# Four layers on one core: the first layer prepared two chunks ahead, norm weights folded, and the feed-forward taps split

## The chip, the cores and the metric

The kernel runs on one core of a Trainium2 chip. A core has five engines that run side by side, each with its own queue: TensorE (PE in the profile, its weight loads PEld), VectorE (DVE), ScalarE (ACT), GpSimd (POOL) and SyncE (SP), which here only starts DMAs. The metric is device time in microseconds, the median of several runs.

## The reference

The input x has shape (4, 64, 128, 128): 4 images, 64 channels, 16,384 pixels. It goes through four layers; the change touches the first and the last.

- Layer 0 is a Mamba block over all 65,536 pixels as one sequence, with 128 inner channels and 16 states, then a linear layer, a norm over the channels, SiLU, and x added.
- Layer 1 is a windowed transform with a small two-layer product in it; layer 2 is two convolutions with a gate.
- Layer 3 is two convolutions, a Mamba block for each image with 64 states between two norms, and a feed-forward part (FFN): 64 to 256 channels, a 3x3 convolution on each channel, GELU, and back to 64.

The Mamba step, cut from the reference:

```python
dA = jnp.exp(d_t[..., None] * A)
h = h * dA + (d_t * u_t)[..., None] * b_t[:, None, :]
y = jnp.einsum('bdn,bn->bd', h, c_t)
```

Around it: xz = norm(t) W; a causal convolution of four taps over the sequence and SiLU give u (the kernel's `xc`); z goes through SiLU and gates y (`sz`); delta, B and C are linear in u, delta with a softplus. In layer 3 the norms have weights and biases: norm(t) = (t - mean) * rstd * ln_w + ln_b. In the last step of layer 3, t + FFN(norm(t)) is formed.

## The kernel before

All in float32. The class `_Mamba` (L144) does the scans of layers 0 and 3.

**Tiling of a scan.** The sequence is cut into chunks of 1,024 tokens (`TC`), 64 chunks in either layer. Channels and states are split: 4 states times 32 channels fill the 128 partitions, so a chunk takes 4 channel quarters (`ND`) times 4 groups of states in layer 0, or times 16 in layer 3. Each (group, quarter) is one iteration: 16 or 64 a chunk. `run` (L412) walks over them in order, and `pin` (L269) ties every engine to that order, so within the two Mamba parts each engine's queue is the order of the program text.

**One iteration.** ACT makes `da` = exp(A * `dl`) (L545), three iterations ahead. The input `bx` lies in PSUM, in two buffers. A group of kind "A" gets it from PE, as eight transposes (L485) of `bxT`, which ACT builds in 28 small multiplications a group (L378) and POOL in one block (L382). A group of kind "D" gets it from DVE (L576), as `du` times B, which PE has spread over the partitions (L491). DVE scans (L582), POOL multiplies by C (L585, `cb`), and PE sums over the states into `y` (L404), two iterations after the group's last scan. Layer 0 has the kinds "DADA", layer 3 "DADAADAADADAADAA".

**Feeds.** What a chunk needs besides is written as generators that `beside` (L465) moves on between iterations. A feed yields "piece" where it has work for PE, of which every iteration's budget allows so many; "wait" k to start k iterations later; or "at" an iteration of its own, which layer 0 gives for each step in the table `slots` (L637), counted from the chunk's first iteration. All pieces of feeds go through one PSUM tile, `pm` (one buffer, L241).

- `ahead`, then `inputs` (L293): in layer 3 first the norm (L1299 to L1320); then z into `sz`, and the convolution and SiLU into `xc`.
- `prepare` (L309): v (delta before softplus, four ACT operations), C (to memory, from which `_C` loads `cb`), B, u, step (three products each half that add up delta, which goes to memory `d2` with delta times u, `dus`), duT (its transposes).
- `replicated` (L493): loads `dl` (five buffers) and `du` (one for each quarter) from `d2`, each spread over the partitions by four DMAs, as soon as their tiles are free. All DMAs stand in SyncE's one queue.
- `behind`: gates y with `sz` into `yg` (L608, on DVE), then the projection, and in layer 3 a norm (L1335 to L1340).

The arguments `leads` of `run` tell how many iterations before its chunk `ahead` and `prepare` start: 28 and 16 in layer 0 (L721), 64 and 36 in layer 3 (L1346). Short-lived tiles share the tag "tmp", six buffers (L290).

**The feed-forward part** (`layer3_ffn`, L1350) goes over 32 strips of 16 rows and is not pinned: the order on each engine is chosen when the program is built, from the program order and dependences. For a strip n, DVE makes nine taps of the 3x3 convolution for channels 128 to 255 (`g1`, L1447 to L1453), GELU follows on ACT (L1454); PE makes the first 128 channels with diagonal weights (`pd`, L1464). Between three taps of PE, `first` (L1390) makes a third of the next strip's hidden channels: PE into `ph` (one buffer, L1417), ACT into `h` (L1422), first t = 0 (PE's channels), then t = 1 (DVE's). Then come the output products (`po`, one buffer, L1483 and L1486) and the sums on DVE (L1490).

## Time and profile before

| what | value |
|---|---|
| median of 3 runs | 19,794.03 us (19,793.55 to 19,795.57) |
| the profiled execution, its time | 19,772.88 us |
| its span in the profile | 19,770.9 us |
| granted TensorE clock | 0.88 |
| busy: PE, DVE, ACT, POOL | 77%, 81%, 75%, 72% of the span |
| layer 0 | 0 to 3,800 us |
| layers 1 and 2, layer 3's convolutions | 3,800 to 6,360 us |
| layer 3's Mamba part | 6,360 to 18,530 us |
| feed-forward part | 18,530 to 19,771 us |
| scans (L582), all | 5,120; 2.34 us each |
| POOL's products (L585), all | 5,120; 2.38 us each |

The profile is of one execution. Its parts are: busy time of each engine; the span in 40 slices; the chain that ended last; groups of equal instructions with their busy time, mean duration, the idle time of their engine ahead of them and who ended it; and DMA issues. An idle engine that is not the bound costs nothing by itself. What follows goes by stage, since each has another limit.

### The profile page before, as it was taken

To read this page: it belongs to the slowest core of one execution; us is meant where nothing else is said; L and a number is where in the kernel's file an instruction comes from. 1 tells how busy PE (TensorE), PEld (TensorE's weight loads), DVE (VectorE), ACT (ScalarE), POOL (GpSimd) and SP (SyncE) were. 2 spreads that over 40 slices of the span, in tenths; PEclk is the share of its full clock that TensorE was granted. 3 is DMA by queue.
4 is the path that set the end of the run, shared out by engine and by line. 5 is a ranking of instruction groups with operands and counts; after the bars stand their busy time and mean duration, and the time that the engine had idled before them with its cause. 6 is when DMAs were issued, how large, how long until landed. Compare 5 with 4: busy or idle time off the path is not lost. (4 is left out here: it accounts for less than half of the span.)

```text
span 19770.9 us, 239165 instructions
## 1 busy us (share of the span) xinstructions
PE 15212.0 (77%) x80176; PEld 7692.9 (39%) x80176; DVE 15957.5 (81%) x8862; ACT 14860.6 (75%) x30365; POOL 14218.6 (72%) x8094
## 2 busy tenths in 40 slices
PE   7787877778897777777777777777777777777777
PEld 3333333367544333333333333333333333333222
DVE  6888888722122999999999999999999999999766
ACT  7888888501223988989889888898988999889522
POOL 6888888600000999999899999999999999889400
PEclk8888888879998888888888888888888888888899
DMA  5555555401122233232332323323233232332211
GB/s 132 146 148 144 149 143 150 129 20 43 32 69 70 75 86 88 75 86 76 86 88 76 86 76 86 88 76 86 76 86 88 76 87 79 83 87 75 58 44 41
DMA packets 669526, 1722.92 MB, mean 87 GB/s; under 512 B 196784, under 2 KB 231936, under 8 KB 660864
## 3 DMA queue, kind: packets, MB, share of 16 engines
q1 hardware_dynamic: 668288, 1707.62, 32.7%
q8 instruction: 629, 10.31, 0.2%
q14 instruction: 609, 4.99, 0.1%
HBM read 1434.27 MB, written 272.63 MB: 86 GB/s over the span
## 5 line engine op out<-in xcount | busy, mean ns | idle before, releaser
L585 POOL TENSOR_TENSOR ring<-ring,cb 128x1024 f32<-128x1024 f32 x5120 | 12094.2, 2382 | 1370.7 <-DVE ring L582 1008.9
L582 DVE TENSOR_TENSOR_SCAN ring<-da,state,bx 128x1024 f32<-128x1024 f32 x4848 | 11133.8, 2334 | 805.6 <-PE bx L485 518.7
L545 ACT ACTIVATE da<-dl,A 128x1024 f32<-128x1024 f32 x5120 | 5858.7, 1144 | 1340.4 <-DVE ring L582 727.7
L378 ACT ACTIVATE bxT<-duT,BT 128x128 f32<-128x128 f32 x21504 | 6758.8, 387 | 0.0
L485 PE MATMUL bx<-cst,bxT 128*128 128x128 f32 x24576 | 4311.6, 329 | 2148.4 <-DVE bx L576 1440.6
L485 PEld LDWEIGHTS bx<-cst,bxT 128*128 128x128 f32 x24576 | 3664.2, 215 | 3975.1 <-DVE ring L582 1603.8
L404 PE MATMUL y<-ring,cst 128*32 128x512 f32 x20480 | 3746.6, 641 | 619.1 <-POOL ring L585 618.0
L576 DVE TENSOR_TENSOR bx<-du,bx 128x1024 f32<-128x1024 f32 x2048 | 2515.1, 1228 | 225.2 <-PE bx L491 89.5
L404 PEld LDWEIGHTS y<-ring,cst 128*32 128x32 f32 x20480 | 572.3, 111 | 2246.1 <-POOL ring L585 1391.1
L1134 PE MATMUL cv<-img,cw 64*64 64x512 f32 x9216 | 1009.5, 595 | 76.7 <-DMA img<-d_x 45.7
L491 PE MATMUL bx<-xc,spread 128*128 128x512 f32 x2048 | 1017.1, 619 | 1.3 <-DVE ring L582 0.7
L1065 POOL TENSOR_TENSOR xs<-xs,cl 128x1024 f32<-128x1024 f32 x32 | 74.9, 2340 | 1078.2 <-DVE cl L1064 1078.2
L1408 POOL MEMSET h<- 128x18 f32 x64 | 8.2, 131 | 1135.3 <-DVE g L1451 795.4
L382 POOL TENSOR_TENSOR bxT<-duT,BT 128x512 f32<-128x512 f32 x768 | 803.5, 1046 | 9.3 <-ACT duT L361 9.3
L1295 POOL MEMSET X<- 64x1 f32 x4 | 0.4, 96 | 1125.9 <-DMA cw<-in_l_conv_wT 1125.9
L1134 PEld LDWEIGHTS cv<-img,cw 64*64 64x64 f32 x9216 | 504.0, 134 | 580.1 <-issue 466.3
L1464 PE MATMUL pd<-h,diag 64*64 64x512 f32 x4608 | 665.4, 624 | 0.7 <-issue 0.7
L582 DVE TENSOR_TENSOR_SCAN ring<-da,bx 128x1024 f32<-128x1024 f32 x272 | 609.6, 2276 | 63.1 <-PE bx L485 46.2
L491 PEld LDWEIGHTS bx<-xc,spread 128*128 128x128 f32 x2048 | 347.9, 189 | 693.8 <-DVE ring L582 385.1
L1451 DVE SCALAR_TENSOR_TENSOR g<-h,dww,g 128x2048 f32<-128x2048 f32 x256 | 601.9, 2351 | 9.2
L1422 ACT ACTIVATE h<-ph,ff_fc_b 128x384 f32<-128x384 f32 (+1 forms) x384 | 199.7, 573 | 541.6 <-PE ph L1417 524.1
L250 PE MATMUL pm<-xc,wC 128*32 128x512 f32 (+1 forms) x512 | 190.2, 832 | 515.7 <-ACT pos L316 513.3
(310 smaller groups left out, 13397.9 us busy)
## 6 DMA issues: line engine op xcount, KB each, us to landing
cb<-c SPq DMA_DIRECT2D x5120, 128.0 KB, 2.8
dl<-d SPq DMA_DIRECT2D x2048, 128.0 KB, 4.4
du<-d SPq DMA_DIRECT2D x2048, 128.0 KB, 4.4
d<-pos SPq DMA_DIRECT2D x128, 512.0 KB, 2.6
d<-dus SPq DMA_DIRECT2D x128, 512.0 KB, 3.0
X<-d_t SPq DMA_DIRECT2D x124, 256.0 KB, 5.3
S<-in_x SPq DMA_DIRECT2D x120, 256.5 KB, 4.9
res<-in_x SPq DMA_DIRECT2D x128, 128.0 KB, 2.9
```

The source lines that it names most:

```text
L378: nc.scalar.activation(t[:, k, q].rearrange("p e j -> p (e j)"), c["duT"][:, k, :], AF.Copy, scale=c["BT"][:, k, n : n + 1])
L382: nc.gpsimd.tensor_mul(t[:, k].rearrange("p q e j -> p q (e j)"), c["duT"][:, k].unsqueeze(1).to_broadcast(shape), c["BT"][:, k, NQ * g : ...
L404: nc.tensor.matmul(c["y"][DD * j : DD * (j + 1), _COLS[h]], K.sel, hc[:, _COLS[h]], start=False, stop=u["g"] == self.ng - 1,)
L485: nc.tensor.transpose(bx[:, P * k : P * (k + 1)], v["bxT"][:, k, :, :, j].rearrange("p q e -> p (q e)"), self.K.eye)
L491: nc.tensor.matmul(bx[:, k], self.spread[v["g"]], v["c"]["xc"][:, k], start=True, stop=True)
L545: nc.scalar.activation(das[nexp], v["c"]["dl"][k], AF.Exp, scale=self.A[:, k, v["g"] : v["g"] + 1])
L576: nc.vector.tensor_mul(bxs[i], u["c"]["du"][j], u["B"])
L582: nc.vector.tensor_tensor_scan(hs, das.pop(i), bxs.pop(i), 0.0 if u["c"].get("reset") else st, ALU.mult, ALU.add)
L585: nc.gpsimd.tensor_mul(hc, hs, u["cb"])
L1134: nc.tensor.matmul(p[i][half[h]], W[half[i], k, :], src[half[i], at : at + 4, dx : dx + WW], start=k == 0, stop=k == 8,)
L1451: nc.vector.scalar_tensor_tensor(g1, tap, wk, g1, ALU.mult, ALU.add)
L1464: nc.tensor.matmul(pd[i][half[h]], diag[half[i], k, :], h0[half[i], r : r + 4, dx : dx + WW], start=k == 0, stop=k == 8,)
```

## The change

**First layer.** `leads` become 45 and 25, and the table of slots is spread anew, so that `prepare` of a chunk runs from 24 to 7 iterations ahead of it, and `inputs` from 43 ahead. Two preparations can now be under way, so `front` becomes a table, and `ahead` of a chunk is ended before that of the next starts. `sz` has four buffers in place of three, "tmp" five in place of six.

**Both Mamba parts.** In `prepare`, B stands after the step instead of before u, and duT follows without a wait of two iterations. `dus` goes into the tile of `u`.

**Norms of layer 3.** The weight of the first norm is applied as scale where ACT copies the centred values, its bias goes through the weights once (`shift`) into the biases of SiLU; where the sequence starts, the two columns of padding hold minus the bias. Weight and bias of the second norm go into the feed-forward part's f1 and b1, once. So L1316 and L1340 go.

**Feed-forward part.** `first` makes t = 1 before t = 0. The taps are a generator: five of the next strip's stand before this strip's outputs, four behind, and the GELU of `g1` stands behind the first half of PE's channels.

```diff
@@ -214,7 +214,7 @@
             nc.sync.dma_start(cols[k], w[k])
-        self.conv_b, self.dt_b = cols["conv_b"], cols["dt_b"]
+        self.conv_b, self.dt_b, self.z_b = cols["conv_b"], cols["dt_b"], 0.0
         self.dD = cp.tile([P, P], F32, name="dD")
@@ -238,6 +238,15 @@
+    def shift(self, b):
+        for k, ws in (("conv_b", self.taps), ("z_b", [self.wz])):
+            pm, col = self.pm(), self.cp.tile([P, 1], F32, name=f"{k}_shift")
+            for i, wt in enumerate(ws):
+                self.nc.tensor.matmul(pm[:, :1], wt, b, start=i == 0, stop=i == len(ws) - 1)
+            self.nc.vector.tensor_scalar(col, pm[:, :1], getattr(self, k), None, ALU.add)
+            setattr(self, k, col)
     def pm(self):
@@ -287,13 +296,13 @@
     def tmp(self, name):
-        return self.wp.tile([P, TC], F32, name=name, tag="tmp", bufs=6)
+        return self.wp.tile([P, TC], F32, name=name, tag="tmp", bufs=self.bufs["tmp"])
...
         nc = self.nc
-        xc, sz = c["xc"], c["sz"] = [self.t(k, self.bufs) for k in ("xc", "sz")]
+        xc, sz = c["xc"], c["sz"] = [self.t(k, self.bufs[k]) for k in ("xc", "sz")]
         yield self.slot(c, "z")
@@ -303,7 +312,7 @@
         nc.scalar.activation(xc, pm, AF.Silu, bias=self.conv_b)
-        nc.scalar.activation(sz, sz, AF.Silu)
+        nc.scalar.activation(sz, sz, AF.Silu, bias=self.z_b)
         nc.scalar.preload_act_table_set(SET6)
@@ -328,16 +337,6 @@
-        yield self.slot(c, "B")
-        BT = c["BT"] = self.wp.tile([P, NB, nst], F32, name="BT", tag="BT")
-        block = [
-            (lambda pm, k=k: pm[:, nst * k : nst * (k + 1)], xc[:, P * k : P * (k + 1)], self.wbc[:, :nst], True, True)
-            for k in range(NB)
-        ]
-        pm = yield from self.piece(block[: NB // 2], block[NB // 2 :])
-        nc.scalar.copy(BT.rearrange("p k n -> p (k n)"), pm[:, : nst * NB])
         yield self.slot(c, "u")
@@ -347,10 +346,20 @@
         nc.sync.dma_start(d2[0], pos)
-        du = self.tmp("dus")
+        du = u
         nc.gpsimd.tensor_mul(du, pos, xc)
         nc.sync.dma_start(d2[1], du)
-        yield self.slot(c, "duT", 2)
+        yield self.slot(c, "B")
+        BT = c["BT"] = self.wp.tile([P, NB, nst], F32, name="BT", tag="BT")
+        block = [
+            (lambda pm, k=k: pm[:, nst * k : nst * (k + 1)], xc[:, P * k : P * (k + 1)], self.wbc[:, :nst], True, True)
+            for k in range(NB)
+        ]
+        pm = yield from self.piece(block[: NB // 2], block[NB // 2 :])
+        nc.scalar.copy(BT.rearrange("p k n -> p (k n)"), pm[:, : nst * NB])
+        yield self.slot(c, "duT")
@@ -514,19 +523,21 @@
         first, second = {}, {}
+        at = -1
         for c in chunks[1:]:
-            at = max(0, per * c["no"] - leads[0])
+            at = max(at + 1, per * c["no"] - leads[0])
             first[at] = c
             second[max(at + 8, per * c["no"] - leads[1])] = c
-        front, early = None, {}
+        front, early = {}, {}
         for i, (u, j) in enumerate(its):
             if i % per == per - 4:
-                finished(front)
+                finished(front.get(u["c"]["no"] + 1))
                 replicated(i - 1)
...
                 finished(early[second[i]["no"]])
-                front = started(self.prepare(second[i]), i)
+                front[second[i]["no"]] = started(self.prepare(second[i]), i)
             if i in first:
+                finished(early.get(first[i]["no"] - 1))
                 early[first[i]["no"]] = started(ahead(first[i]), i)
@@ -634,9 +645,9 @@
     nc = tc.nc
-    slots = {"v": -16, "C": -15, "B": -14, "u": -13, "step": -8, "duT": -6, "z": -23, "conv": -21}
-    slots |= {"project": 21, "rstd": 23, "store": 29}
-    m = _Mamba(ctx, tc, K, 16, w, "DADA", 3, slots)
+    slots = {"z": -43, "conv": -37, "v": -24, "C": -22, "u": -21, "step": -16, "B": -14, "duT": -7}
+    slots |= {"project": 22, "rstd": 23, "store": 29}
+    m = _Mamba(ctx, tc, K, 16, w, "DADA", {"xc": 3, "sz": 4, "tmp": 5}, slots)
     cp, wp = m.cp, m.wp
@@ -718,7 +729,7 @@
     chunks = [{"at": divmod(i * TC, HW), "reset": i == 0} for i in range(B * HW // TC)]
-    m.run(chunks, ahead, behind, (28, 16), [12] * 16)
+    m.run(chunks, ahead, behind, (45, 25), [12] * 16)
@@ -1267,21 +1278,25 @@
     nc = tc.nc
-    m = _Mamba(ctx, tc, K, 64, w, "DADAADAADADAADAA", 2)
+    m = _Mamba(ctx, tc, K, 64, w, "DADAADAADADAADAA", {"xc": 2, "sz": 2, "tmp": 6})
     cp = m.cp
...
     nc.sync.dma_start(woT, w["out_wT"])
-    g1, b1, g2, b2 = (_dup(nc, cp, w[k], f"{k}_") for k in ("ln1_w", "ln1_b", "ln2_w", "ln2_b"))
-    def centred(x, out):
+    g1, b1 = (_dup(nc, cp, w[k], f"{k}_") for k in ("ln1_w", "ln1_b"))
+    m.shift(b1)
+    pad = cp.tile([P, 1], F32, name="pad")
+    nc.vector.tensor_scalar_mul(pad, b1, -1.0)
+    def centred(x, out, scale=1.0):
...
         )
-        nc.scalar.copy(out[0], pm[:, :w])
+        nc.scalar.activation(out[0], pm[:, :w], AF.Copy, scale=scale)
         nc.scalar.activation(out[1], pm[:, :w], AF.Square)
@@ -1304,20 +1319,18 @@
         else:
-            nc.gpsimd.memset(S[:, :2], 0.0)
+            nc.gpsimd.tensor_copy(S[:, :2], pad.to_broadcast([P, 2]))
         xs, sq = m.tmp("nxc"), m.tmp("nsq")
-        yield from centred(c["X"], (xs, sq))
+        yield from centred(c["X"], (xs, sq), g1)
         if c is not chunks[-1]:
...
         yield from m.rstd(sq, eps)
-        nc.gpsimd.tensor_mul(xs, xs, sq)
+        nc.gpsimd.tensor_mul(S[:, 2:], xs, sq)
+        if not t0:
+            nc.gpsimd.tensor_copy(S[:64, 2:3], pad[:64])
+        nc.gpsimd.tensor_copy(tail, S[:, TC:])
         yield "wait", 2
-        nc.vector.tensor_scalar(S[:, 2:], xs, g1, b1, ALU.mult, ALU.add)
-        if not t0:
-            nc.gpsimd.memset(S[:64, 2:3], 0.0)
-        nc.gpsimd.tensor_copy(tail, S[:, TC:])
-        yield "wait", 1
         yield from m.inputs(c, S)
@@ -1336,8 +1349,7 @@
         nc.gpsimd.tensor_mul(o, xs, o)
-        yield "wait", 2
-        nc.vector.tensor_scalar(o, o, g2, b2, ALU.mult, ALU.add)
+        yield "wait", 3
         for h in range(NH):
@@ -1377,6 +1389,13 @@
     nc.sync.dma_start(b1, w["fc1_b"].rearrange("(t q) o -> q (t o)", t=2))
+    g, n = (_dup(nc, cp, w[k], f"ff_{k}") for k in ("ln2_w", "ln2_b"))
+    ph = hp.tile([P, 2, 4, WW], F32, name="ph", tag="ph")
+    for t in range(2):
+        nc.tensor.matmul(ph[:, t, 0, :1], f1[half[0], t, :], n[half[0]], start=True, stop=True)
+    nc.vector.tensor_add(b1, b1, ph[:, :, 0, 0])
+    nc.vector.tensor_scalar(f1, f1, g, None, ALU.mult)
     dwb1 = cp.tile([P, 1], F32, name="dwb1")
@@ -1403,7 +1422,7 @@
         yield
-        for t in range(2):
+        for t in (1, 0):
             himg = H[t] = wp.tile([P, R + 2, RW], F32, name=f"h{t}", tag=f"h{t}")
@@ -1431,17 +1450,8 @@
         pass
-    for n, (b, r0) in enumerate(strips):
-        simg = s3[b].rearrange("c (r w) -> c r w", w=WW)
-        oimg = out[b].rearrange("c (r w) -> c r w", w=WW)
-        h0, h1 = H[0], H[1]
-        H = {}
-        ahead = first(*strips[n + 1], H) if n + 1 < len(strips) else iter(())
-        next(ahead, None)
-        res = wp.tile([P, NK, 4, WW], F32, name="res3", tag="res3")
-        for q in range(R // 4):
-            nc.sync.dma_start(res[half[q % 2], q // 2], simg[:, r0 + 4 * q : r0 + 4 * q + 4, :])
+    def taps(h1):
@@ -1451,7 +1461,22 @@
                 nc.vector.tensor_scalar(g1, tap, wk, None, ALU.mult)
-        nc.scalar.activation(g1, g1, AF.Gelu, bias=dwb1)
+            if k in (4, 8):
+                yield g1
+    for g1 in taps(H[1]):
+        pass
+    for n, (b, r0) in enumerate(strips):
+        simg = s3[b].rearrange("c (r w) -> c r w", w=WW)
+        oimg = out[b].rearrange("c (r w) -> c r w", w=WW)
+        h0 = H[0]
+        H = {}
+        ahead = first(*strips[n + 1], H) if n + 1 < len(strips) else iter(())
+        next(ahead, None)
+        res = wp.tile([P, NK, 4, WW], F32, name="res3", tag="res3")
+        for q in range(R // 4):
+            nc.sync.dma_start(res[half[q % 2], q // 2], simg[:, r0 + 4 * q : r0 + 4 * q + 4, :])
@@ -1472,8 +1497,13 @@
                 nc.scalar.activation(g0[i][:, kk], pd[i], AF.Gelu, bias=dwb[:, i : i + 1])
+            if not kk:
+                nc.scalar.activation(g1, g1, AF.Gelu, bias=dwb1)
         for _ in ahead:
             pass
+        later = taps(H[1]) if H else iter(())
+        g2 = next(later, None)
@@ -1492,6 +1522,8 @@
             nc.sync.dma_start(oimg[:, r0 + 4 * q : r0 + 4 * q + 4, :], o[half[q % 2], q // 2])
+        next(later, None)
+        g1 = g2
```

## The prediction

> **What bounds the kernel now.** I read the stage windows first, because the layers have different limits. An "iteration" below is one scan of 1,024 tokens (L582); layer 0 has 16 per chunk, layer 3 has 64, and there are 64 chunks in each. Columns: window, its length, busy time of PE, PEld, DVE, ACT, POOL.
>
> ```profile
> 0.00:3800.00 3800.00, 2998.06 (x13698) 1399.12 (x13698) 3105.12 (x1679) 3132.67 (x5762) 3031.38 (x1668) 0.87 0.56 143
> ...
> 6360.00:18530.00 12170.00, 9108.58 (x44212) 4598.20 (x44212) 11498.87 (x5884) 10885.08 (x23404) 11023.77 (x6208) 0.88 0.31 82
> 18530.00:19771.00 1241.00, 970.67 (x6164) 289.02 (x6164) 746.66 (x444) 339.37 (x550) 16.71 (x148) 0.90 0.18 43
> ```
>
> Layer 0 is bound by no engine: all four are at about 80%, so hand-offs set it. From 100 to 3560 us a chunk takes 58.0 us. Layer 3's Mamba part takes 190 us a chunk and VectorE is busy 94%. The feed-forward part (FFN) takes 37.57 us a strip (gelu L1454 starts at 18927.12 and again at 18964.68) with PE at 78% and DVE at 60%: a chain sets it. Layers 1 and 2, 3,800 to 6,360 us, are untouched. Idle times "at iteration n" are those of the trace, put to the scan that had started last and averaged over the chunks.
>
> Layer 0, the waits from 100 to 3560 us (us in total, times, longest), then its timeline near 3696 us:
>
> ```profile
> DVE ring L582 <- PE bx L485: 258.0, 141, 18.7
> DVE yg L608 <- remote: 223.4, 58, 4.9
> ...
> ACT da L545 <- DMA dl<-d: 173.7, 102, 3.2
> ```
>
> ```profile
> 3695.40 1.07 PE L250 MATMUL pm<-xc,wC 128*32 128x512 f32 x2 [7.21 <-ACT pos L316]
> ...
> 3696.28 2.74 PE L404 MATMUL y<-ring,cst 128*32 128x512 f32 x6
> ...
> 3699.10 1.23 DVE L608 TENSOR_TENSOR yg<-y,sz 128x1024 f32<-128x1024 f32 x1 [4.11 <-remote]
> ```
>
> At the chunk boundary the C matmul stands in PE's queue until ACT has emptied the single `pm`; the last y sums stand behind it; `yg` waits for them, and the scans stand behind `yg`. The "remote" wait is thus PE's y sums: 223.4 / 58 = 3.85 us a chunk.
>
> Layer 3, groups by line from 7,000 to 18,000 us (58 chunks; after the bar: busy us, mean ns, idle before and who ended it), of DVE and of ACT, then SyncE's queue and ACT at one boundary:
>
> ```profile
> L1316 DVE TENSOR_SCALAR S<-nxc,ln_w__37414,ln_b__37417 128x1024 f32<-128x1024 f32 x58 | 117.1, 2020 | 0.0
> ...
> L1340 DVE TENSOR_SCALAR o<-o,ln_w__37420,ln_b__37423 128x512 f32<-128x512 f32 x58 | 30.3, 522 | 0.0
> ```
>
> ```profile
> L545 ACT ACTIVATE da<-dl,A 128x1024 f32<-128x1024 f32 x3708 | 4243.5, 1144 | 1008.2 <-DVE ring L582 625.7 <-DMA dl<-d 342.2 <-DVE bx L576 33.9
> ```
>
> ```profile
> 12250.58 8.09 SPq L507 DMA_DIRECT2D du<-d  x16
> 12258.80 1.89 SPq L507 DMA_DIRECT2D dl<-d  x4
> ```
>
> ```profile
> 12264.82 1.15 ACT L545 ACTIVATE da<-dl,A 128x1024 f32<-128x1024 f32 x1 [4.08 <-DMA dl<-d]
> ```
>
> `delta` (`pos`) is written out only at iteration 54 (12242.85 us here, L349), so sixteen `du` loads stand ahead of the `dl` loads that the next chunk's first exponentials need. ACT loses 342.2 / 58 = 5.9 us, and then runs without a pause from iteration 2 to 19, where DVE waits.
>
> FFN, one strip:
>
> ```profile
> 18927.12 2.00 ACT L1454 ACTIVATE g<-g,dwb 128x2048 f32<-128x2048 f32 x1 [8.92 <-DVE g L1451]
> ...
> 18930.11 1.65 PE L1417 MATMUL ph<-N,f 64*128 64x384 f32 x4 [6.69 <-ACT h L1422]
> ...
> 18941.14 1.28 DVE L1453 TENSOR_SCALAR g<-h,dww 128x2048 f32<-128x2048 f32 x1 [14.05 <-ACT h L1422]
> ```
>
> The loop is closed: nine taps on DVE, gelu on ACT, the eviction of `h` that stands behind it, PE, the last `h` of t=1, and only then the next taps: 23.5 + 14.05 us.
>
> [...]`e` with a bias column takes 1.09 us from PSUM against 0.99 us for a plain copy. So Copy with scale g1 in place of the copy L1284 costs 0 to 0.1 us. I take 0.
>
> **Layer 0, two chunks ahead.** No instruction is removed from the loop except that `du` reuses `u`. What moves, by iteration of the 16: v 0 to 8, C 1 to 10, u 3 to 11, step 8 to 0, B stays at 2, duT 10 to 9, z 9 to 5, conv stays at 11, project 5 to 6.
> - `yg`: at iteration 0 there is now the step. Its matmuls took 5.4 us (12 of 0.6, overlapping). They fit in iterations 0 to 1 (3.7 us each, D groups, where DVE makes its own input), and the y sums at 1 and 2 stand before B, so they end some 8 us after the boundary; `yg` comes at 9.8. Gain 3.84. This cover is thin, 2 us.
> - Of the 258.0 us that scans wait for transposes, 0.8 us a chunk falls at iteration 4, 1.1 at 5, 2.2 at 13. The first goes with the stall. The second is y's start (L401, 3.3 us of PE) ahead of iteration 5's transposes: stays.
> - At 8 to 11 v, duT, C and conv now take turns in the one `pm`. ACT gets e, pos, exp and ln (4.2 us) there in place of two copies (2.0), C's copy 0.6 and the copy of duT as before. I follow PE and ACT one behind the other: conv ends about 1.2 us later than now, with transposes and scan of iteration 13 behind it. The u op (0.67 us of DVE) moves into that wait: net +0.6.
> - The five `dl` and four `du` tiles are asked for earlier; SyncE issues the same number. 0; it helps ACT by up to 2.9 us (173.7 / 60), which is not on the path.
>
> Sum -3.84 - 0.8 + 0.6 = -4.0 us a chunk, times 62 = -250. The first two chunks now crowd iterations 0 to 12 with two preparations: +15, an estimate from three extra pieces of some 5 us. Layer 0: **-235**. Bounds: +1 us a chunk if the crowding costs all of it, -5.5 if every wait goes: +80 to -350.
>
> **Layer 3, norms in weights.** L1316 and L1340 go: (117.1 + 30.3) / 58 = 2.54 us of DVE a chunk. POOL's multiply writes S directly (2.39 us as before); the pad columns cost 0.2 us at each image's start. These ops lie where ACT is the bound, so alone they would give nearly nothing (ACT waits for DVE only 0.35 us at iterations 8 and 9). But B is now behind the step: in D groups the budget is 2, 2, 2, 1 pieces and 0 in A groups. C is done at 34, so the six pieces of the step fall on 40 to 42 instead of 52 to 54, and B and duT on 43 to 53 (duT was forced at 60). `delta` is out 27 us earlier: each `du` goes when its tile falls free (52 to 55) and the `dl` loads follow the exponentials of 60 to 62 directly, issue 2 + landing 4.4 us, in time. ACT gets its 5.9 us back. DVE's idle time is (437.3 + 119.2 + 30.3) / 58 = 10.1 us; some 3.2 are 0.1 us hand-offs in the 24 D iterations, 2.4 lie at 4 and 5, 2.0 at 13 to 19. I take 3.0 of these last 4.4 as gone. -2.54 - 3.0 = -5.5, times 63 = **-347**. Bounds: -0.5 (ACT still the bound) to -8 (DVE's 177 + 5): -30 to -510.
>
> **FFN.** t=1 first; five of the next strip's taps stand before this strip's outputs, four behind. Then gelu of g1 needs only taps that ended early in the strip, and PE runs on. PE's floor: six blocks of 24 depthwise and 4 `ph` matmuls at 3.58 us (starts 18913.45, 18917.03) and two groups of `po` at some 2.8 (18901.99 to 18904.9): 27.1 us. DVE: 1.29 + 8 x 2.36 + 4 x 0.75 = 23.2 us, below. `po` has one buffer: its second group waits for two outputs (1.5 us) that may stand behind half a tap (1): 29.6 us. -8.0 x 31 = -248, +10 for the first strip's full taps: **-238**. The order here is not pinned but chosen when the program is built; bounds 27.1 to 36.2 a strip: -320 to -40. The scaling of f1 and b1, and `shift`: four small loads, four matmuls of one column and some DVE ops once, +5.
>
> Sum: -235 - 347 - 238 + 5 = -815. From the span of 19,770.9: 18,956. The profiled execution itself took 19,772.88 us, the median of the runs is 21 above that, 23 above the span: **18,980 us**.
>
> **Rivals.**
> 1. All of it comes, at the lower bounds of two layers: -350 - 510 - 300 = 18,635. For it: the idle ACT time. Against: all engines then stand above 90%.
> 2. Layer 3's gain is hidden: `dl` still late, because SyncE's queue waits long for `cb` buffers (POOL state, 14.2 us at the longest) and `dl` stands behind. -30 instead of -347: 19,297.
> 3. FFN's order puts all nine taps ahead of the outputs: 20.2 + 1.5 + 2.8 + three blocks 10.7 + 1.0 = 36.2 us; 19,175.
> 4. Layer 0's crowding at 8 to 13 costs the 4 us again: 19,215.
> 5. Slower: with five `tmp` buffers for six a chunk, the `l` of the chunk after next could take the buffer of `du`, which now lives until duT. ACT's ln then waits for PE's transposes, with all exponentials and bxT behind it, PE waiting for the same `pm`. Before shows no such wait; the code's order says a few us. It decides only from (235 + 580) / 64 = 12.7 us a chunk; at 14 us the result is 19,877.
>
> **How the numbers follow.** Forecast 0.50 (18,830 to 19,130); rival 1 0.13; 2 0.13; 3 0.10; 4 0.07; 5 0.07, of which 0.02 near no change. The range 18,660 to 19,330 leaves out half of rival 1, rival 5, and tails. Runs agree within 0.01%; 0.2% (40 us) is taken as what a measurement tells from no change. Faster 0.93, same 0.02, slower 0.05.
>
> **What would show it.** Right: `yg`'s wait below 1 us; layer 0 near 54 us a chunk; ACT's wait for `dl` in layer 3 near 0 and its chunk near 184.5; no rows L1316 and L1340; strips near 30 us. Wrong: `yg` waiting for a DMA or POOL; scans at iteration 13 waiting over 4 us; ACT's ln idle before it; a strip above 35.

## The result, and the profile after

| | before | after |
|---|---|---|
| median of 6 runs | 19,793.79 us (19,779.98 to 19,799.98) | 19,722.35 us (19,695.11 to 19,736.35) |
| profiled execution, span | 19,772.88, 19,770.9 us | 19,736.35, 19,734.5 us |

The ratio is 0.9963, 95% interval 0.995 to 0.9976: 0.37% faster, 71 us, where 814 us were forecast. The time lies far outside the range, which ended at 19,330. By stage, between the two profiled executions (layer 0 ends with its last scan, layer 3's Mamba part runs from its first scan to its last):

| stage | before | after | change | forecast |
|---|---|---|---|---|
| layer 0 | 3,790 | 3,662 | -128 | -235 |
| layers 1, 2, convolutions of 3 | 2,588 | 2,564 | -24 | 0 |
| layer 3, Mamba part | 12,146 | 12,211 | +64 | -347 |
| feed-forward part | 1,246 | 1,298 | +52 | -238 |

The -24 in the second row is not the change's: a later run of the kernel before with one edit in layer 3 (e11_move_alone, below) took 2,567 us there.

The stage windows of after (window, length, busy time of PE, PEld, DVE, ACT, POOL, granted clock, DMA share, GB/s):

```profile
0.00:3662.00 3662.00, 2887.52 (x13678) 1392.77 (x13682) 3117.07 (x1678) 3129.64 (x5766) 3037.51 (x1664) 0.90 0.57 149
...
6226.00:18437.00 12211.00, 9295.00 (x44186) 4609.49 (x44190) 11359.83 (x5757) 10948.82 (x23391) 10989.09 (x6202) 0.86 0.30 81
18437.00:19734.00 1297.00, 978.12 (x6182) 291.38 (x6174) 748.49 (x446) 343.37 (x550) 21.87 (x150) 0.86 0.16 42
```

In layer 3 DVE is busy for less time than before, and the stage is longer. TensorE's clock is higher in layer 0 (0.90 for 0.87) and lower in layer 3 (0.86 for 0.88) and in the feed-forward part (0.86 for 0.90).

**Layer 0**, 100 to 3560 us: DVE's waits (us in total, times, longest), then its timeline round one `yg` and at iterations 11 to 13 of the chunk before it.

```profile
DVE ring L593 <- PE bx L494: 265.6, 182, 8.3
DVE bx L587 <- PE bx L500: 91.3, 62, 1.5
```

```profile
2881.17 1.98 PE L494 MATMUL bx<-cst,bxT 128*128 128x128 f32 x8
2882.94 4.47 PE L259 MATMUL pm<-S,cw 128*128 128x512 f32 x8
...
2887.25 2.10 PE L494 MATMUL bx<-cst,bxT 128*128 128x128 f32 x16
2888.48 6.82 DVE L593 TENSOR_TENSOR_SCAN ring<-da,state,bx 128x1024 f32<-128x1024 f32 x3 [1.46 <-PE bx L494]
...
2906.44 1.20 DVE L619 TENSOR_TENSOR yg<-y,sz 128x1024 f32<-128x1024 f32 x1
```

A wait "at iteration n" is idle time of DVE just ahead of scan n of a chunk, counted from 0, or behind that scan ahead of DVE's other work. `yg` waits for nothing now: the 3.85 us are back. The chunk is 56.03 us for 58.02, since other waits grew: iteration 5 has 1.73 us, 7 has 1.77 (the spread products L500 stand behind z and the projection, a new wait), 12 and 13 have 2.58 together. At 13 the convolution's eight products stand between two bursts of transposes.

**Layer 3**, 7,000 to 18,000 us: ACT's exponentials, the loads at one chunk's end, DVE's waits.

```profile
L556 ACT ACTIVATE da<-dl,A 128x1024 f32<-128x1024 f32 x3687 | 4228.6, 1147 | 1110.7 <-DVE ring L593 1107.2
```

```profile
11896.55 0.34 SPq L348 DMA_DIRECT2D d<-pos  x1
...
11937.58 1.70 SPq L516 DMA_DIRECT2D dl<-d  x4
11941.23 3.62 SPq L516 DMA_DIRECT2D dl<-d  x8
```

```profile
DVE ring L593 <- PE bx L494: 425.9, 382, 2.4
DVE bx L587 <- PE bx L500: 113.9, 230, 0.7
```

The step moved as forecast: `delta` goes out at 11,897, 58 us ahead of the next chunk's first scan (11,954), the loads follow as buffers fall free, and nothing waits for `dl` any more. But ACT's idle time a chunk is the same, 19.50 us for 19.64: what it lost to `dl` it now waits for DVE (1107.2 for 625.7 in the window). And the scans wait longer for transposes: 425.9 us for 256.8.

| layer 3, us a chunk (mean of 61) | chunk | DVE busy | DVE idle |
|---|---|---|---|
| before | 189.96 | 179.79 | 10.17 |
| after | 190.98 | 177.63 | 13.35 |

**Feed-forward part**, one strip of after, DVE, PE and the GELU of `g1`:

```profile
18935.25 19.13 DVE L1461 SCALAR_TENSOR_TENSOR g<-h,dww,g 128x2048 f32<-128x2048 f32 x8
...
18943.03 1.08 PE L1513 MATMUL po<-g,f 128*64 128x512 f32 x4
...
18954.41 1.53 DVE L1520 SCALAR_TENSOR_TENSOR o<-po,fc2b__124169,res 64x512 f32<-64x512 f32 x2
18954.47 2.00 ACT L1501 ACTIVATE g<-g,dwb 128x2048 f32<-128x2048 f32 x1 [9.96 <-DVE g L1461]
...
18956.00 1.97 PE L1513 MATMUL po<-g,f 128*64 128x512 f32 x4 [9.18 <-DVE o L1520]
...
18973.75 1.28 DVE L1463 TENSOR_SCALAR g<-h,dww 128x2048 f32<-128x2048 f32 x1 [10.59 <-ACT h L1441]
```

All nine taps stand ahead of the strip's outputs. The first group of `po` is ready at 18,946 and DVE takes it at 18,954; PE stands 9.18 us, because `po` has one buffer, and comes back slower: its granted clock is 0.50 from 18,956 to 18,960 us, and the same four products take 1.97 us for 1.08. A strip takes 38.6 to 39.8 us in turn.

### The profile page after: what moved, and what is told of

It reads as the page before. It is cut to its first block, busy times and chain, and to the rows that moved or that the text cites. A ratio compares the mean times of both kernels' runs of the same rounds, so it can differ in the third digit from the quotient of the medians.

```text
span 19734.5 us, 238606 instructions
## 1 busy us (share of the span) xinstructions
PE 15294.8 (78%) x80186; PEld 7627.5 (39%) x80186; DVE 15836.0 (80%) x8739; ACT 14933.8 (76%) x30369; POOL 14205.9 (72%) x8094
## 5 line engine op out<-in xcount | busy, mean ns | idle before, releaser
L494 PE MATMUL bx<-cst,bxT 128*128 128x128 f32 x24576 | 4458.7, 338 | 2842.8 <-DVE bx L587 2053.0
L494 PEld LDWEIGHTS bx<-cst,bxT 128*128 128x128 f32 x24576 | 3743.1, 214 | 4917.0 <-DVE bx L587 2068.7
L413 PE MATMUL y<-ring,cst 128*32 128x512 f32 x20480 | 3566.6, 660 | 332.4 <-POOL ring L596 332.2
L413 PEld LDWEIGHTS y<-ring,cst 128*32 128x32 f32 x20480 | 532.3, 112 | 1735.7 <-POOL ring L596 856.1
L500 PE MATMUL bx<-xc,spread 128*128 128x512 f32 x2048 | 1018.0, 620 | 1.4
L1145 PEld LDWEIGHTS cv<-img,cw 64*64 64x64 f32 x9216 | 437.2, 134 | 643.5 <-issue 568.0
L500 PEld LDWEIGHTS bx<-xc,spread 128*128 128x128 f32 x2048 | 347.7, 189 | 687.7 <-issue 464.1
```

The source lines that it names most:

```text
L413: nc.tensor.matmul(c["y"][DD * j : DD * (j + 1), _COLS[h]], K.sel, hc[:, _COLS[h]], start=False, stop=u["g"] == self.ng - 1,)
L494: nc.tensor.transpose(bx[:, P * k : P * (k + 1)], v["bxT"][:, k, :, :, j].rearrange("p q e -> p (q e)"), self.K.eye)
L500: nc.tensor.matmul(bx[:, k], self.spread[v["g"]], v["c"]["xc"][:, k], start=True, stop=True)
L1145: nc.tensor.matmul(p[i][half[h]], W[half[i], k, :], src[half[i], at : at + 4, dx : dx + WW], start=k == 0, stop=k == 8,)
```

## The experiments

Stages do not overlap in time, so a kernel can carry an edit in each. Every run's stages, in us (chunks: mean):

| run | layer 0, chunk | layer 3, chunk | feed-forward | whole |
|---|---|---|---|---|
| before | 58.02 | 189.96 | 1,246 | 19,773 |
| after | 56.03 | 190.98 | 1,298 | 19,736 |
| e1_ffn_old | 55.95 | 190.81 | 1,252 | 19,678 |
| e2_ffn_order | 55.97 | 190.40 | 1,173 | 19,568 |
| e3_l3_warm | 55.91 | 201.39 | 1,300 | 20,411 |
| e4_l3_same_work | 56.02 | 190.40 | 1,299 | 19,697 |
| e5_l3_b_first | 55.89 | 190.65 | 1,299 | 19,707 |
| e7_l0_z | 56.32 | 190.81 | 1,298 | 19,751 |
| e8_ffn_order2 | 55.95 | 190.81 | 1,057 | 19,495 |
| e9_l3_warm | 56.00 | 218.29 | 1,299 | 21,488 |
| e6_l3_budget | 56.02 | 195.76 | 997 | 19,743 |
| e10_warm_ffn3 | 58.09 | 189.96 | 999 | 19,504 |
| e11_move_alone | 58.01 | 193.50 | 1,243 | 19,968 |
| e12_first_pieces | 61.44 | 187.49 | 998 | 19,547 |
| e13_parts | 56.02 | 187.32 | 998 | 19,207 |
| e14_y_early | 56.54 | 187.62 | 998 | 19,271 |

### The feed-forward part: what stands behind what

The theory: the place of the taps, of the outputs and of one GELU in DVE's and ACT's queues sets the strip. The rival: the clock, or the folded weights.

**e1_ffn_old** puts the loop of before back and leaves the rest.

```diff
-        for t in (1, 0):
+        for t in range(2):
...
-        later = taps(H[1]) if H else iter(())
-        g2 = next(later, None)
```

> The feed-forward loop of before (t = 0 first, nine taps and their GELU ahead of PE's channels) in the kernel after; norms stay folded. Theory (the loss in this part comes from the order in which VectorE got the taps and the outputs): the part takes 1,246 us again instead of 1,298, a strip 37.6 us instead of about 39.5. Rival (the part is longer because TensorE's granted clock was lower, 0.86 for 0.90, or because the weights are folded): it stays above 1,280 us.

Measured: 1,252 us, strips of 37.7. So the loop is what lost; folding the norm costs at most some 6 us once. The granted clock of this part is 0.90 again, as in before: it followed the loop.

**e2_ffn_order** ties DVE's instructions of a strip to the order of the program text.

```diff
+            if i.engine == nc.vector.engine:
+                if prev[0]:
+                    tc.add_manual_dep(i, prev[0], ..., reason="order")
+                prev[0] = i.name
...
         g1 = g2
+        pin()
```

> The kernel after, with VectorE's instructions of the feed-forward loop tied to the order of the program text: five taps, the four outputs, four taps. Theory: outputs no longer stand behind all nine taps, po's second group comes early and TensorE runs on; a strip takes 28.5 to 31 us, the part 960 to 1,020 us, the whole about 19,430. Rival (the order of taps and outputs is not what holds TensorE; GELU of g1 or the single buffer of ph does): a strip stays above 36 us.

Measured: 1,173 us, strips of 34.9 to 36.9, between the two. The outputs came early, and a new wait took the place (timeline of one strip):

```profile
18971.65 9.58 DVE L1461 SCALAR_TENSOR_TENSOR g<-h,dww,g 128x2048 f32<-128x2048 f32 x4
18981.33 2.00 ACT L1518 ACTIVATE g<-g,dwb 128x2048 f32<-128x2048 f32 x1 [17.43 <-DVE g L1461]
18981.63 1.65 PE L1436 MATMUL ph<-N,f 64*128 64x384 f32 x4 [5.58 <-DVE N L1416]
```

GELU of `g1` needs the four late taps and stands in ACT's queue ahead of the evictions of `ph` (the copies out of PSUM into `h`); all of the next strip's hidden channels stand behind it. (This strip is at an image's border, where PE also waits for N's zero row, L1416, which stands behind the same taps.)

**e8_ffn_order2** ties ACT too, and puts that GELU last.

```diff
-            if not kk:
-                nc.scalar.activation(g1, g1, AF.Gelu, bias=dwb1)
         for _ in ahead:
             pass
+        nc.scalar.activation(g1, g1, AF.Gelu, bias=dwb1)
```

> The kernel after; in the feed-forward loop VectorE and ScalarE are both tied to the order of the program text, and GELU of g1 is put behind all of the strip's other ScalarE work instead of behind the first half. With VectorE alone tied, a strip took about 35.4 us, because GELU of g1 waited for the four late taps at the head of ScalarE's queue with the evictions of ph behind it. Theory: that wait goes, TensorE is held only by its own work, and a strip takes 28 to 31 us, the part 950 to 1,030 us. Rival (the four late taps still end too late for po, or the h evictions are the limit): 33 us or more.

Measured: 1,057 us. An ordinary strip takes 29.5 us; two at each image border take 36.3 and 39.6, since the zero row of N (L1416) stands behind the late taps on DVE. In **e6_l3_budget**, e10, e12, e13 and e14 (whose other edits are below) GpSimd writes that row, and the part takes 997 to 999 us:

```diff
-            nc.vector.memset(N[:64, 0:1, :], 0.0)
+            nc.gpsimd.memset(N[:64, 0:1, :], 0.0)
```

A strip of e13_parts, which has the same loop:

```profile
18701.97 1.53 DVE L1535 SCALAR_TENSOR_TENSOR o<-po,fc2b__124169,res 64x512 f32<-64x512 f32 x2 [2.90 <-PE po L1531]
...
18708.11 9.58 DVE L1461 SCALAR_TENSOR_TENSOR g<-h,dww,g 128x2048 f32<-128x2048 f32 x4
...
18717.61 1.28 DVE L1463 TENSOR_SCALAR g<-h,dww 128x2048 f32<-128x2048 f32 x1
...
18726.38 2.02 ACT L1518 ACTIVATE g<-g,dwb 128x2048 f32<-128x2048 f32 x1
...
18728.45 1.08 PE L1528 MATMUL po<-g,f 128*64 128x512 f32 x4 [1.48 <-ACT g L1518]
```

Outputs at 18,702, four taps, no pause, five taps, and PE waits 1.48 us a strip, for the GELU of `g1`; its clock is 0.98 in this stage. The strip of 29.5 us has the length that the prediction had worked out (29.6), but is made up otherwise, as is told below.

### Layer 3: the clock, the order, and one place in TensorE's queue

DVE lost 2.2 us of work a chunk and got 3.2 us of waiting. **e5_l3_b_first** and **e11_move_alone** part the two edits, the folded norms and the move of B and duT in `prepare`. The first keeps the norms folded and sets `prepare` back, the second does only the move in the kernel before.

```diff
# e5_l3_b_first; e11_move_alone is the reverse, on before
+        if not self.slots:
+            yield self.slot(c, "B")
...
         yield self.slot(c, "u")
...
-        yield self.slot(c, "duT")
+        yield self.slot(c, "duT", 2)
```

> The kernel after, with layer 3's prepare in the order of before (B ahead of u, duT with its wait of two); the first layer and the folded norms stay. Theory (the earlier step frees ACT of the dl wait, but lets TensorE run out of work in the D groups, which costs more): ACT waits for dl again, some 5.9 us a chunk, and yet the chunk is shorter than the 191.1 us of after: 188 to 190 us. Rival (folding the norms, not the move, made layer 3 longer): 191 us or more, with both losses.

> The kernel before, with only layer 3's prepare in the order of after: B behind u and the step, duT without its wait. The norms stay on VectorE. The norms alone, with the order of before, gave 190.65 us a chunk where before has 189.96. Theory (the move does what was forecast of it and frees ACT of the dl wait, but TensorE's idle stretches take the gain): ACT's dl wait is near 0 and the chunk is 189 to 191.5 us. Rival (the move gains when VectorE keeps its norm work, because its longer chunk hides TensorE): 186 to 188.5 us.

| us a chunk | chunk | DVE busy | DVE idle |
|---|---|---|---|
| norms alone (e5) | 190.65 | 177.50 | 13.15 |
| move alone (e11) | 193.50 | 180.85 | 12.65 |

Both chunks are longer than the theories had it (e5's by a little, between theory and rival). ACT's waits in e5 show `dl` late again, 316.6 us in the window (before: 342.2), and the chunk hardly differs from after:

```profile
ACT da L567 <- DVE ring L604: 664.5, 1086, 3.3
ACT da L567 <- DMA dl<-d: 316.6, 125, 5.7
```

So the `dl` wait costs nothing that something else does not cost. Folding the norms gave its 2.3 us of DVE and 3.0 us of new waiting; the move alone costs 3.5 us a chunk. "The move loses and the norms gain" is thereby no explanation: each alone makes DVE wait about as long as both. Small differences say nothing here: the runs that leave layer 3 as in after (e1, e2, e7, e8) have 190.40 to 190.81 us a chunk, and after 190.98. Of the move's 3.5 us, 2.5 are waiting; the rest is longer work of DVE, since `u` takes 2.82 us for 0.67 and the norm's L1316 0.79 for 2.02, for a reason that no run here shows.

What waits? In the trace of before, PE and the scans at iterations 10 to 13 of a chunk:

```profile
12114.03 1.98 PE L250 MATMUL pm<-S,cw 128*128 128x512 f32 x4
...
12117.72 1.23 PE L485 MATMUL bx<-cst,bxT 128*128 128x128 f32 x8 [1.70 <-DVE bx L576]
12117.76 6.82 DVE L582 TENSOR_TENSOR_SCAN ring<-da,state,bx 128x1024 f32<-128x1024 f32 x3
12118.88 1.07 PE L250 MATMUL pm<-tr,cst 128*64 128x512 f32 x2
12119.79 1.02 PE L250 MATMUL pm<-yg,woT 128*64 128x512 f32 x2
12120.74 1.23 PE L485 MATMUL bx<-cst,bxT 128*128 128x128 f32 x8
```

and of after:

```profile
11992.15 1.98 PE L494 MATMUL bx<-cst,bxT 128*128 128x128 f32 x8 [3.99 <-DVE bx L587]
...
11994.06 1.97 PE L259 MATMUL pm<-tr,cst 128*64 128x512 f32 x2
...
11995.83 1.91 PE L259 MATMUL pm<-yg,woT 128*64 128x512 f32 x2
...
11997.67 2.37 PE L494 MATMUL bx<-cst,bxT 128*128 128x128 f32 x16
...
11999.18 4.59 DVE L593 TENSOR_TENSOR_SCAN ring<-da,state,bx 128x1024 f32<-128x1024 f32 x2 [2.40 <-PE bx L494]
```

The work is the same. In before the convolution's products fall on iterations 9 and 10, and PE stands idle 1.70 us ahead of the transposes, of which each scan of an A group needs a burst of eight. In after S is ready earlier, they fall on 8 and 9, and PE stands 3.99 us. Then its granted clock is 0.50 (11,992.1 to 11,998.0 us; in before 1.00 from 12,117.7 to 12,124.0). The transposes take 1.98 us for 1.23, and the projection, which stands between the first and the second burst, 1.97 and 1.91 us for 1.07 and 1.02; the second burst begins 5.5 us after the first in place of 3.0, and the scan of iteration 13 waits 2.40 us. Over the chunks the idle stretch at this place is 1.86 us in before and 3.97 in after.

The move brings this, not the folded norms. In after and in e11 the norm's own product on TensorE, which S waits for, comes at iteration 1, in before and e5 at 2 and 3. With the norms alone (e5) the convolution lies mainly on iteration 9, the idle stretch is 2.90 us and the scans wait 0.92 us at 13. With the move alone (e11) the products lie as in after, the stretch is 4.06 us and the wait 2.23, although the trace puts more than half of it (1.24 us) down to ACT's `bxT`:

```profile
12381.12 1.98 PE L495 MATMUL bx<-cst,bxT 128*128 128x128 f32 x8 [3.82 <-DVE bx L586]
...
12383.03 1.97 PE L250 MATMUL pm<-tr,cst 128*64 128x512 f32 x2
...
12384.79 1.92 PE L250 MATMUL pm<-yg,woT 128*64 128x512 f32 x2
...
12386.64 2.46 PE L495 MATMUL bx<-cst,bxT 128*128 128x128 f32 x16
```

TensorE's pace changes so all through layer 3. In after, from 7,000 to 18,000 us, bursts of eight behind 3.5 us or more of idle time have a median of 1.56 us from first start to last, and 0.94 behind less than 1 us. The granted clock in the traces of before and after is either 1.00 or 0.50, and in the same window the bursts that lie wholly at 0.50 (342) have a median of 1.56 us, those wholly at 1.00 (806) of 0.94. The idle stretch ahead does not settle which it is: the bursts that follow scan 43, behind some 3.55 us, mostly take 0.91, at a clock of 1.00.

There are two suspects, then: the clock, and the piece that stands between the bursts.

**The clock.** e3_l3_warm, e9_l3_warm and e10_warm_ffn3 add products in the D groups that break TensorE's idle stretches there, e4_l3_same_work is the control. The products of e3 and e4 go to `pm` and nobody reads them; those of e9 and e10 multiply by zeros into sums (in e10's first group into `pm`). What the kernel computes is unchanged.

```diff
# e3_l3_warm (e4_l3_same_work: j in (0,), range(4))
+            if self.nst == 64 and u["kind"] == "D" and j in (1, 2) and not holding():
+                pm = self.pm()
+                for _ in range(2):
+                    nc.tensor.matmul(pm[:, :512], self.K.eye, hs[:, :512], start=True, stop=True)
# e9_l3_warm
+            for _ in range(warm.get(j, 0) if "y" in yc else 0):
+                nc.tensor.matmul(yc["y"][:, _COLS[1]], self.none, hs[:, :512], start=False, stop=False)
# e10_warm_ffn3
+                for _ in range(2 if u["g"] else 3):
+                    nc.tensor.matmul(to, self.none, das[i + 3][:, :512], start=not u["g"], stop=not u["g"])
```

> The kernel after; in layer 3's D groups, where TensorE stands idle, two products of 512 columns that nobody reads are added at the second and third iteration of each group[...]. Theory (after its idle stretches TensorE runs at a lower clock, and the transposes that follow come late to the scans): bursts of eight transposes fall from 1.56 to 0.95 us, layer 3's chunk from 191.0 to 187 to 188.5 us (-160 to -250 us in all). Rival (VectorE's waits come from the order of the work alone): 191 us or more, because TensorE has more to do.

> Control of the run before it: the same number of added products that nobody reads (four in a D group), but all at the first iteration of the group, so that the idle stretch ahead of the next A group stays. Theory of the clock: no gain, 190.5 to 192 us a chunk in layer 3. Rival (added products help in another way, or the share of busy time in the whole layer sets the clock): as much gain as in the run before it.

> As the earlier run with added products in layer 3's D groups, but they now multiply by zeros into the open sum y, so that they never wait for the one pm buffer, and each waits only for the scan of its iteration: three at the second and two at the third iteration of a group (four at the second in a chunk's first group). The result stays what it was. Theory (TensorE's clock after idle stretches[...] is what costs): bursts of eight transposes after a D group take about 1.0 us for 1.56 (chip time from first to last), and the chunk falls from 191.1 to between 186 and 188.5 us. Rival (the order of work alone): 191 us or more.

e3 and e9 failed as tests. `hs` overlaps the columns that GpSimd writes next, so each added product waited for GpSimd (in e3 17.2 us of PE's time a chunk; in e9 1,306.0 us from 7,000 to 18,000 us, in 303 waits), and sums and transposes stood behind it in PE's queue. e4 is at the value of after; its median chunk is 191.13 us. But it holds an undesigned test. Its first chunks run at 187.7 us and the later ones at 191.1, with the same instructions (six chunks each; columns as in the stage windows, the clock is the third number from the end):

```profile
6598.00:7725.00 1127.00, 851.44 (x4155) 421.39 (x4156) 1065.87 (x542) 1028.98 (x2200) 1032.51 (x583) 0.90 0.31 83
12864.00:14011.00 1147.00, 874.96 (x4155) 433.37 (x4156) 1067.06 (x541) 1029.19 (x2198) 1031.90 (x583) 0.86 0.30 82
```

All engines do the same; TensorE's clock is 0.90 or 0.86, and the chunk goes with it. The waits at iterations 39, 47 and 59 (3.0 us together) are there only in the second; that the clock makes them is argued from this, not shown, since a slower rhythm could also give TensorE more idle time and so the lower clock. e2_ffn_order, which leaves layer 3 alone, has such a stretch too: the schedule of after holds itself in one rhythm or the other.

> The kernel after with added products that multiply by zeros in the D groups of both Mamba parts. They read the newest exponential (da) of ScalarE, so that they come one iteration apart and wait for nothing on GpSimd; two at the second and two at the third iteration into the open y, and in a chunk's first group three at the third iteration into pm. The result stays what it was. The earlier run of this kind read the scan's output, which overlaps what GpSimd writes, and each waited for it; its bursts of eight transposes were all at 0.94 us, as the theory of the clock has it, while the waits cost 27 us a chunk. Theory: now the bursts are near 0.94 us without the waits; layer 3's chunk falls from 191.1 to between 186 and 188.5 us, layer 0's from 55.7 to between 53 and 55. Rival (the cold clock costs nothing that the order would not cost anyway): 190.5 us or more and 55.5 or more. The feed-forward part is as in the run before: 985 to 1,010 us.

In e10 the wait for GpSimd is gone and the clock is 0.92 in layer 3. At the place shown above TensorE is idle for 0.52 us, the second burst begins 3.02 us after the first with the projection still between them, and the wait at 13 is 0.00. The chunk is 189.96 us, most chunks still at 191.1. Scans wait for transposes 243.7 us in the window for 425.9, but DVE now waits 113.9 us for ACT's `bxT`, which in after it hardly did, and 50.2 for `da` (23.7). In layer 0 the same edit made the wait at iteration 12 3.60 us for 0.88 and the chunk 2.1 us longer. So a higher clock by added work (0.92 for 0.86) gives back at most 1 us of a chunk: the next engine's wait takes the place. The clock is a part of the loss, and keeping it up by added products is no cure.

**The piece.** A D group's fourth iteration may take one piece, which then stands between the two bursts.

```diff
-    ... ([2, 2, 2, 1] if k == "D" else [0] * ND)
+    ... ([1, 2, 2, 2] if k == "D" else [0] * ND)   # e6_l3_budget
+    ... ([3, 2, 2, 0] if k == "D" else [0] * ND)   # e12_first_pieces
```

> The kernel after with two edits in different stages. Layer 3: the budget of pieces in a D group becomes 1, 2, 2, 2 in place of 2, 2, 2, 1, so that TensorE's products lie later in the group and less idle time stands ahead of the next group's transposes. Theory of the idle stretches: the chunk falls from 191.1 to between 187.5 and 190 us. Rival (no gain, since the late pieces stand ahead of the transposes): 191 us or more. Feed-forward part: VectorE and ScalarE tied as before, and the zero border of N moves from VectorE, where it stood behind the four late taps, to GpSimd. Expected there: the strips at image borders fall from 36.3 and 39.6 us to about 29.5 and the part takes 985 to 1,010 us.

Wrong in sign: 195.76 us. Scans waited for transposes 673.5 us in the window. At iteration 13 the edit did what it was made for: the idle stretch is 0.66 us and the wait 0.00. But the waits at 5, 16 and 51 grew from 1.73, 0.01 and 0.57 us to 4.02, 3.24 and 2.66. That suggested the opposite edit.

> The kernel after with one edit in each stage. Layer 3: budget of pieces in a D group 3, 2, 2, 0 in place of 2, 2, 2, 1, since a piece at the fourth iteration stands in TensorE's queue between the transposes of the next group's first two scans; with 1, 2, 2, 2 the chunk had become 4.4 us longer. Theory: the wait at iteration 13 (2.3 us) goes and with it those that the clock makes at 39, 47 and 59: 186 to 189 us a chunk for 191.0. Rival (the first iterations are the tight ones; or the idle stretch only grows, and the clock with it takes the gain): 190.5 us or more. Layer 0: the projection, its norm and the store two iterations later (24, 25, 31 for 22, 23, 29), out of the way of iteration 7's spread products. Theory: the wait at iteration 7 (1.77 us) goes, 54 to 55 us a chunk; rival (the work only meets v, C and conv at 8 to 13): 55.7 or more. Feed-forward part as in the two runs before it: 997 to 999 us. All three as the theories have it: 19,170 to 19,320 us; if only the feed-forward part gains: 19,430.

Layer 3: 187.49 us, the theory's number, by half of its mechanism. The wait at 13 went, and those at 19 and 31 fell from 1.05 us each to 0.10 and 0.39; those at 39, 47 and 59, which were to go with it, stayed (2.99 us in after, 2.83 here). At the same place in e13_parts, with the same budget:

```profile
11884.25 1.98 PE L494 MATMUL bx<-cst,bxT 128*128 128x128 f32 x8 [3.96 <-DVE bx L587]
11884.30 9.07 DVE L593 TENSOR_TENSOR_SCAN ring<-da,state,bx 128x1024 f32<-128x1024 f32 x4
11886.70 1.58 PEld L494 LDWEIGHTS bx<-cst,bxT 128*128 128x128 f32 x8 [0.87 <-DVE ring L593]
11886.70 1.98 PE L494 MATMUL bx<-cst,bxT 128*128 128x128 f32 x8 [0.47 <-DVE ring L593]
```

TensorE is still idle 3.96 us and still slow, 1.98 us for a burst, and four scans run without a pause. The projection has gone to iteration 19. What costs is the piece between two bursts at a moment when TensorE is slow (in after a burst of 1.98 us and 2.40 us of waiting at 13); without the piece the slow burst costs nothing at this place (e12 and e13, wait 0.00), and behind an idle stretch of only 0.52 us the piece costs nothing there (e10, wait 0.00). The clock over layer 3 stays 0.86, DVE's idle time is 9.87 us a chunk and its work 177.46: the 2.3 us that the norms freed now come out as 2.6.

DVE's waits by place, us a chunk (mean of 60 chunks):

| iterations | 4, 5 | 7 | 13 | 14 to 19 | 39, 47, 59 |
|---|---|---|---|---|---|
| before | 2.38 | 0.32 | 0.41 | 1.55 | 0.64 |
| after | 1.73 | 0.10 | 2.30 | 1.06 | 2.99 |
| norms alone (e5) | 2.49 | 2.83 | 0.92 | 1.27 | 0.59 |
| move alone (e11) | 1.96 | 0.10 | 2.23 | 0.84 | 1.32 |
| e12 | 1.66 | 0.10 | 0.00 | 1.07 | 2.83 |
| e13 | 1.58 | 0.10 | 0.00 | 1.16 | 2.17 |

### Layer 0: waits that change places

**e7_l0_z** moves z to iterations 2 and 3, where TensorE stands idle.

```diff
-    slots = {"z": -43, "conv": -37, ...
+    slots = {"z": -46, "conv": -37, ...
-    m.run(chunks, ahead, behind, (45, 25), [12] * 16)
+    m.run(chunks, ahead, behind, (47, 25), [12] * 16)
```

> The kernel after, with the first layer's z three iterations earlier (leads 47 and slot -46 in place of 45 and -43), so that z's products fall on iterations 2 and 3, where TensorE stands idle 4.5 us, and no longer ahead of the spread products and transposes of iterations 5 to 7. Theory: VectorE's waits at iterations 5 (1.73 us) and 7 (1.77 us) fall by 2 to 3.5 us together and the chunk goes from 55.7 to between 52.5 and 54 us (-110 to -200 us in all). Rival (those waits come from y's start and from the clock alone): 55.5 us or more.

56.32 us, the rival's side, though not for its reason. The waits for transposes and spread products fall from 265.6 and 91.3 us to 127.9 and 47.3, and a new one stands beside them: `DVE ring <- ACT sz`, 198.6 us, 3.3 a chunk at iteration 5.

**e12_first_pieces** also moved the projection, norm and store two iterations later. The wait at 7 fell from 1.77 to 0.76 us, but the chunk rose to 61.44: at 13 to 15, where v, C and the convolution stand, DVE waits 8.4 us. The rival was right.

### Together

**e13_parts**: after, with budget 3, 2, 2, 0 and the tied feed-forward loop. **e14_y_early** besides starts y ahead of the first transposes of a chunk, where TensorE is idle.

```diff
                 full = None
+            first_y = u["g"] == 0 and i == u["last"] and not full and not owed
+            if first_y:
+                self._sums(u, None)
             produced(i + 1)
```

> The kernel after with the two edits that gained, and the first layer as the change has it: layer 3's budget 3, 2, 2, 0 (187.5 us a chunk in the run before), and the feed-forward loop with VectorE and ScalarE tied, GELU of g1 last and N's border on GpSimd (998 us). Theory (the stages do not touch one another, and these two causes carry what the forecast missed): layer 0 near 3,660 us, layer 3 near 11,990, together 19,220 us, between 19,190 and 19,250. Rival (layer 3's gain came with the late first layer of that run, or with the clock that it left): layer 3 at 12,150 us or more and the whole above 19,350.

> As the run beside it, with the start of y (16 products into the new sum) ahead of the next group's first transposes in a chunk's first group, where TensorE stands idle (4.5 us in layer 0, 5.65 us in layer 3), in place of between the first and the second transposes. Both reasons given for the wait at iteration 5 are tested: if y's place in TensorE's queue makes it (1.7 us in layer 0 and 1.7 in layer 3), it goes, and the shorter idle stretch leaves the clock up: layer 0 from 55.7 to 54 to 55.2 us a chunk, layer 3 from 187.5 to 185 to 186.8 us, together -60 to -200 us. Rival (y's start then makes the first transposes late by as much, since y is free only after yg): no change within 30 us, or slower.

e13_parts: 19,207.26 us, ratio to before 0.971 (0.9695 to 0.9724), with the stages as expected (3,660, 2,567, 11,982, 998; sum 19,207). It is faster than both kernels; the layer 3 gain of e12 did not hang on its first layer. e14_y_early: 19,271.02 us, 0.9742 (0.9726 to 0.9759), slower than e13. In layer 3 the wait at iteration 5 goes, and one of 1.74 us at iteration 4 comes, of which 1.37 is for ACT's `bxT`; in layer 0 likewise (1.63 us at 4). y's place made the first wait, and another stood right behind.

## Why the prediction was wrong, step by step

**Layer 0.** Right: `yg` (-3.84) and the stall at iteration 4 (-0.8) went. Wrong in size: the wait at 5 was to stay at 1.1 us and is 1.73, those at 12 and 13 were to cost 0.6 more and cost 0.4; the one at 7 (1.77 for 0.17) was not foreseen, though the prediction lists z at 5 and project at 6, which stand ahead of the spread products of the next D group. It counted what a moved product does to `pm` at 8 to 13 and not what it does at 5 to 7. Moving z (e7) or the projection (e12) away brings this wait down to 0.78 or 0.76 us. Together -2.0 us a chunk in place of -4.0. The +15 us at the start did not show: -128 is 62 chunks of -2.0 and about -4.

**Layer 3, the norms.** The step "-2.54" was right as work: DVE has 2.2 us less in after, 2.3 in e5 alone, and the Copy with scale costs ACT 1.09 us for 0.99, within the 0 to 0.1 us that were put. That "alone they would give nearly nothing" held too: e5's chunk is 0.7 us longer than before's. The 3.0 us of new waiting that the norms bring alone lie mostly at iteration 7 (2.83 us for 0.32) and are gone there once the move is added.

**Layer 3, the sum.** The step that failed is "-3.0 stalls ... I take 3.0 of these last 4.4 as gone". DVE's idle time grew by 3.2 us. Of the 4.4 us, the waits at 4 and 5 went from 2.38 to 1.73 us, but those at 13 to 19 rose from 1.96 to 3.36, and those at 39, 47 and 59, which the prediction does not name, from 0.64 to 2.99. It took PE as fast enough wherever DVE was waiting less, and did not ask what the move does to the products that follow S. These come an iteration earlier (in e11 as in after), leave TensorE idle 4 us where it had been idle 1.9, and the projection (1.97 and 1.91 us for 1.07 and 1.02) and the transposes (1.98 for 1.23) then run at a granted clock of 0.50 in one queue. e12 and e13 show what it costs: with the projection out of that place the wait at 13 is 0.00 and the chunk 187.3 to 187.5 us. The same edit moves pieces in all six D groups, so not all of the gain is that one place's. Why the waits at 39, 47 and 59 came, and mostly stayed, is open.

**Layer 3, the move.** Everything that the prediction said of positions came: the step at 39 to 41, `delta` out early, no wait for `dl`. "ACT gets its 5.9 us back" was true and worth nothing: ACT waits for DVE instead, and e5, where `dl` is late again, is no slower than after. The step that failed is the reading of an idle engine's largest wait as the bound. Alone the move costs 3.5 us a chunk (e11), of which 1.8 lie at iteration 13. Not tried, and so open: whether before with the new budget, or the old order of `prepare` with it, does as well as e13.

**Feed-forward part.** "Then gelu of g1 needs only taps that ended early in the strip, and PE runs on" failed: with DVE in the order of the text (e2) that GELU waits for the four late taps, 17.4 us in the strip shown and 7.7 in the mean, and a strip takes some 35 us. Only with ACT tied too and this GELU moved (e8) is it 29.47 us. That this meets 29.6 is in part luck: the 2.5 us that were put for the outputs ahead of `po`'s second group are not there (one wait of 0.8 us in e13), PE waits 1.47 us a strip for the GELU instead, and the rest of the strip, PE's work, is 28.0 us for 27.1. What failed in after itself is the choice of likelihood: "the order here is not pinned" was said, and rival 3, all nine taps ahead of the outputs, was given 0.10; it is what happened. Its size was wrong as well: 36.2 us, while the strip is 39.2. In the strip shown, taps take 20.5 us, PE's restart 1.6, the second group of `po` with the depthwise products among it some 5.6 where 2.8 were put, and the rest to the next first tap 12.1 where 11.7 were put: the missing term is TensorE's slow start after 9.18 us of idleness (granted clock 0.50, four products in 1.97 us for 1.08). With 37.57 us in before, that turns rival 3 from a gain to a loss.

**Rival 5** (ACT's ln held by "tmp") did not show. **The chances** failed where the three gains were held to be likely each by itself; in each stage a change of order, not an amount of work, had to come out as assumed.

## What to carry to other kernels

Before a wait is counted as a gain, find the next wait behind it at the same place: here `dl`, the start of y and z each gave way to another of nearly the same size. A step that comes earlier moves what it feeds; look at what then stands between two items that the critical engine needs from a queue, and move that away (two numbers in a budget were worth some 220 us). Where the order on an engine is chosen by a program builder, read the order in the trace, or tie it, before forecasting from the text.

## What the runs showed of the hardware that was not expected

- One program had two rhythms in one execution: 187.7 and 191.1 us a chunk, granted clock 0.90 and 0.86, changing by itself (in e4 at the 9th, 22nd and 25th chunk) and holding between.
- The stage with the higher clock was not the faster one: e10 has 0.92 in layer 3 and 189.96 us a chunk; e13 has 0.86 and 187.32. In the feed-forward part the clock was higher where PE was idle less: 0.86, 0.92, 0.97 and 0.98 with PE idle for 25, 15, 10 and 8% of the time, in after, e2, e8 and e13 (1,298, 1,173, 1,057 and 998 us).
- Bursts of eight transposes behind 2.5 to 3 us of idle time were already slower, 1.28 us from first start to last in after (1.41 in before), between the 0.94 and 1.56 of the two ends. In e13 the 22 such bursts have 1.56: the last idle stretch alone does not settle the pace.
